# Layer 3's q and k on two 128x64 column tiles of the TensorE array, then copied to the row groups

## The chip, the cores and the metric

The kernel runs on one core of a Trainium2 chip. The metric is the device time of one execution in microseconds (us). The kernel before took 2777.07 us (median of three runs, 2775.02 to 2780.0); the profiled execution has a span of 2772.2 us. On this core TensorE (PE) multiplies, VectorE (DVE) and ScalarE (ACT) do the elementwise work and empty PSUM, GpSimd (POOL) does little, and SyncE (SP) issues nearly all DMAs. Each engine works through its own queue in order.

## The reference

Sixteen images of 256 channels and 32x32 points pass through four layers: a group norm with attention (layer 0), a gate made by two small convolutions (layer 1), group norm with attention again (layer 2), and an attention with narrow q and k (layer 3). All is float32. Layer 3 is the one that changes:

```python
def _L3_conv_ref(x, Wq, bq, Wk, bk, Wv, bv, gamma):
    B, C, H, W = x.shape                       # 16, 256, 32, 32
    N = H * W
    Dqk = Wq.shape[0]                          # 32
    scale = jnp.asarray(Dqk, x.dtype) ** (-0.5)
    xf = x.reshape(B, C, N)
    q = jnp.einsum('qc,bcn->bqn', Wq, xf) + bq[None, :, None]
    k = jnp.einsum('qc,bcn->bqn', Wk, xf) + bk[None, :, None]
    v = jnp.einsum('vc,bcn->bvn', Wv, xf) + bv[None, :, None]
    energy = jnp.clip(jnp.einsum('bqn,bqm->bnm', q, k) * scale, -10.0, 10.0)
    attn = jax.nn.softmax(energy, axis=-1)
    out = jnp.einsum('bcm,bnm->bcn', v, attn).reshape(B, C, H, W)
    return gamma[0] * out + x
```

## The kernel before

**Samples and lanes.** One sample (image) is one pass of the generator `sample`: attention of layer 0, the gate, attention of layer 2, then `clipped_attend`, which is layer 3. Even samples run in lane 0 and odd ones in lane 1. The two lanes are interleaved step by step (each `yield` is a step), with lane 1 a fixed number of steps behind, so that one lane's matrix products fill the waits of the other. The last part of each sample also carries `head` of the sample two further on: loading it and its first group norm (lines 118 to 145, among them two tiny products, `gm` on line 125 and `gv` on line 134, of which `gv` multiplies the small tile `d` from DVE line 131). While an even sample is in `clipped_attend`, lane 1 is in its layer 2; while an odd one is there, lane 0 has begun layer 0 of its next sample (the tiles `t`, lines 599 and 906).

**Order.** A tile framework places the instructions on the engines, keeps their order per engine, and adds the semaphores. It takes two accesses to one tile by different engines to be dependent more often than the data alone would ask. All PSUM tiles of the fast path come from one pool of eight banks (`bank`, 128 x 512 float32 each), used in turn.

**Matmuls in float32.** The trace shows each float32 matmul as two MATMUL records and two LDWEIGHTS records of the same shape; counts of the profile are counts of these records.

**Layer 3's q and k.** `w3` holds Wq, Wk and Wv side by side (columns 0 to 31, 32 to 63, 64 to 319) for the two halves `c` of the channels. At the start `fold3` makes `w3r` out of it, 128 columns wide: Wq twice and Wk twice. For each half `h` of the 1024 points (512 points), two matmuls over `c` on line 1041 (128 rows, 128 columns, 512 points) fill one bank: q in rows 0 to 31 and again in 32 to 63, k in 64 to 95 and again in 96 to 127. Four evictions follow: line 1050 (ACT) writes the 64 rows of q, with bias and scale, into rows 0 to 63 of the tile `t_qk`, then into rows 64 to 127; line 1057 (DVE) does so with k. ACT's and DVE's copies alternate in time, each waiting for the one before. The first copy of a sample also waits for DMA, because `t_qk` lies in the slot `t` of its lane, which the transfers of layer 2's output (`send`, line 515) still read.

So all four row groups of 32 partitions hold all of q and all of k. On line 1074 four products with 32 rows each, one per row group, run beside each other in the array: each takes another 128 keys and all 512 points of the half. ACT exponentiates their results (line 1083) and DVE clips them (line 1086). Between the copies and these products stand the values' products (line 525, evicted by ACT on line 1061) and the other lane's work. Lines 471 (bias strips), 906 (layer 0's `t`), 1061 and 1050 share ACT's queue; 131 (`d`), 136 (`ve`), 599, 638 to 641 (`tc`) and 1057 share DVE's.

Of the kernel before, what the change touches and what calls it, by code (L numbers as in the profile page):

```python
# [10 lines left out]
FP = mybir.dt.float32  # L11
I32 = mybir.dt.int32
AF = mybir.ActivationFunctionType
ALU = mybir.AluOpType
AX = mybir.AxisListType

P = 128
C = 256
CC = C // P
HW = 1024  # L20
NT = HW // P
HALF = 512
NH = HW // HALF
TPH = HALF // P
GROUP = 32
DQK = 32
G4 = P // DQK
PH = P // 2
STRIP = 32
NG = P // STRIP  # L30
# [11 lines left out]
OFFSET = 30  # L42


W_PLANES, W_GATE1, W_GATE2, W_SEND1 = 5, 3, 1, 8
W_NORM1, W_NORM2, W_NORM3, W_SEND2 = 6, 3, 2, 6
W_EXP, W_AV, W_AV3 = 2, 0, 0

S_W1, S_W2, S_B1, S_B2, S_GAMMA, NSCAL = 0, 18, 27, 28, 29, 30

# [150 lines left out]
def fast_path(nc, tc, k, bad, x, w_l0, w_l2, w_l3, qk_bias, v_bias, tap_idx, out):  # L201
# [7 lines left out]
    with ExitStack() as ctx:  # L209
        wts = ctx.enter_context(tc.tile_pool(name="wts", bufs=1))  # L210
# [12 lines left out]
        def bank(nm):  # L223
            return ps_m.tile([P, HALF], FP, tag="m", name=nm)
# [5 lines left out]
        def slot(what, lane, shape, nm):  # L230

            return qkvp.tile(shape, FP, tag=f"{what}_{lane}", name=f"{what}_{nm}", bufs=1)
# [26 lines left out]
        w3 = wts.tile([P, CC, 2 * DQK + C], FP, name="w3")  # L259
# [11 lines left out]
        bcol0, bcol2, bcol3 = (wts.tile([P, CC], FP, name=f"bcol{i}") for i in (0, 2, 3))  # L271
# [1 line left out]
        bstrip0, bstrip3 = (wts.tile([P, NS], FP, name=f"bstrip{i}") for i in (0, 3))  # L273

        qb = wts.tile([P, 1], FP, name="qb")
        for g in range(G4):
            i = g // 2
            nc.sync.dma_start(qb[g * DQK : (g + 1) * DQK, :], qk_bias[i * DQK : (i + 1) * DQK, :])

        def right_sums(engine, w, nm):  # L280

# [91 lines left out]
        def in_strips(col, strips, nm):  # L373

            ps = bank(f"strips_{nm}")
            for s in range(NG):
                nc.tensor.matmul(
                    ps[:STRIP, s * CC : (s + 1) * CC],
                    k.ident[:, s * STRIP : (s + 1) * STRIP],
                    col,  # L380
                    start=True,
                    stop=True,
                )
            for g in range(NG):
                nc.vector.tensor_copy(
                    strips[g * STRIP : (g + 1) * STRIP].rearrange("p (c s) -> p s c", c=CC),
                    ps[:STRIP, :NS].rearrange("p (s c) -> p s c", c=CC),
                )


        w3r = wts.tile([P, CC, P], FP, name="w3r")
        gam = k.sc[:, S_GAMMA : S_GAMMA + 1]

        def fold3():
            for g in range(G4):
                i = g // 2
                tc.keep_in_program_order(
                    nc.gpsimd.tensor_copy(
                        w3r[:, :, g * DQK : (g + 1) * DQK], w3[:, :, i * DQK : (i + 1) * DQK]
                    )  # L400
                )
            ps = bank("bias3")
            for c in range(CC):
                nc.tensor.matmul(
                    ps[:, CC : CC + 1],
                    w3r[:, c, :],
                    bcol2[:, c : c + 1],
                    start=(c == 0),
                    stop=(c == CC - 1),
                )  # L410
            for o in range(CC):
                for c in range(CC):
                    nc.tensor.matmul(
                        ps[:, o : o + 1],
                        w3[:, c, 2 * DQK + o * P : 2 * DQK + (o + 1) * P],
                        bcol2[:, c : c + 1],
                        start=(c == 0),
                        stop=(c == CC - 1),
                    )
            tc.keep_in_program_order(  # L420
                nc.vector.tensor_tensor(qb, ps[:, CC : CC + 1], qb, ALU.add)
            )
            nc.vector.tensor_scalar(qb[:PH], qb[:PH], DQK**-0.5, None, ALU.mult)
            nc.vector.tensor_tensor(bcol3, ps[:, :CC], vcol[:, 2, :], ALU.add)
            nc.vector.scalar_tensor_tensor(bcol3, bcol3, gam, bcol2, ALU.mult, ALU.add)
            in_strips(bcol3, bstrip3, "l3")
# [48 lines left out]
        def turn_strips(y, ts):  # L475

            part = y[:, :, ts].rearrange("p s t j -> p s (t j)")
            nc.vector.transpose(part, part)  # L478

        def by_strips(tokens):  # L480

            return tokens.rearrange("p (t g j) -> p g t j", t=TPH, g=NG)

        def half(h):
            return slice(h * TPH, (h + 1) * TPH)

        def in_pairs(y, ts, bias):

            return [
                functools.partial(add_to_strips, y, ts, bias, slice(s, s + 2))  # L490
                for s in range(0, NS, 2)
            ]
# [279 lines left out]
        def wait(steps):  # L772

            for _ in range(steps):
                yield
# [254 lines left out]
        def clipped_attend(xt, y, lane, b):  # L1030

            qk = slot("t", lane, [P, 2, HW], f"qk3_{b}")
            q, kk = qk[:, 0], qk[:, 1]
            vt = vts[lane]
            for h in range(NH):
                hs = slice(h * HALF, (h + 1) * HALF)
                ps = bank(f"qk3_{b}_{h}")
                for c in range(CC):  # L1040
                    nc.tensor.matmul(
                        ps.rearrange("p (g n) -> p g n", g=TPH),
                        w3r[:, c, :],
                        xt[:, half(h), c],
                        start=(c == 0),
                        stop=(c == CC - 1),
                    )

                for s in (slice(0, PH), slice(PH, P)):
                    nc.scalar.activation(  # L1050
                        by_strips(q[s, hs]),
                        ps[:PH, :].rearrange("p (g t j) -> p g t j", g=NG, t=TPH),
                        AF.Identity,
                        bias=qb[:PH],
                        scale=DQK**-0.5,
                    )
                    nc.vector.tensor_scalar(kk[s, hs], ps[PH:, :], qb[PH:], None, ALU.add)
                yield
                for t2 in range(h * TPH // 2, (h + 1) * TPH // 2):
                    ps, dst = values_of(xt, t2, w3[:, :, 2 * DQK :], vt, f"l3_{b}")  # L1060
                    nc.scalar.activation(dst, ps, AF.Copy, scale=gam)
                    yield
            tv = value_sums(lane)
            yield
            ri = small.tile([P, NT], FP, tag="ri", name=f"ri3_{b}")
            for h in range(NH):
                hs = slice(h * HALF, (h + 1) * HALF)
                e = expp.tile([P, NT, HALF], FP, tag="e", name=f"e3_{b}_{h}")
                for mg in range(NT // G4):
                    ss = [bank(f"s3_{b}_{h}_{mg}_{g}") for g in range(G4)]  # L1070
                    for g in range(G4):
                        mm = mg * G4 + g
                        gs = slice(g * DQK, (g + 1) * DQK)
                        nc.tensor.matmul(  # L1074
                            ss[g],
                            kk[gs, mm * P : (mm + 1) * P],
                            q[gs, hs],
                            start=True,
                            stop=True,
                        )  # L1080
                    for g in range(G4):
                        mm = mg * G4 + g
                        nc.scalar.activation(e[:, mm, :], ss[g], AF.Exp)  # L1083
                        if g % 2:
                            part = e[:, mm - 1 : mm + 1, :]
                            nc.vector.tensor_scalar(
                                part, part, EXP_MIN, EXP_MAX, ALU.max, ALU.min
                            )
                    yield from wait(W_EXP)
                yield from wait(W_AV3)  # L1090
                if b == B - 1 and h == NH - 1:
                    last = combp.tile([P, TPH, C], FP, tag="cb", name="last")
                    yield from weighted(e, vt, tv, y, ri, h, f"l3_{b}", last)
                    store_last(last, b, h)
                    continue
                yield from weighted(e, vt, tv, y, ri, h, f"l3_{b}")
                turn_strips(y, half(h))
                chores[lane].extend(in_pairs(y, half(h), bstrip3))
                chores[lane].append(functools.partial(store_tokens, y, b, h))
                yield  # L1100
            count(ri, f"l3_{b}")
# [59 lines left out]
        ps = bank("badp")  # L1161
# [317 lines left out]
```

## Time and profile before

| what | value |
|---|---|
| time, median of 3 | 2777.07 us |
| span of the profiled execution, granted TensorE clock | 2772.2 us, 0.996 |
| q/k matmuls, line 1041 | 128 records of 592 ns (median) |
| first copy on ACT, line 1050 | 64 x 680 ns |
| k's copy on DVE, line 1057 | 64 x 756 ns |
| products of q and k, line 1074 | 512 records |
| from first q/k matmul to first line-1074 product, even samples / odd samples | about 22.4 / 24.3 us |

A row of the groups gives line, engine, operation, what is written and read with shapes, the number of records, the time in which at least one of them ran, the mean length of one, and the idle time of the engine just before them with what ended it. In the timeline the columns are the start in us, the length of the merged run, engine, line, operation and count, and in brackets the idle time before it with the releaser.

### The profile page before, as it was taken

How to read it: one execution, taken by the hardware profiler on the slowest of the kernel's cores; microseconds unless marked ns; L12 is line 12 of the kernel's file. 1: busy time of each engine (PE TensorE's matmuls, PEld its weight loads, DVE VectorE, ACT ScalarE, POOL GpSimd, SP SyncE). 2: the span in 40 equal slices, each digit the busy share in tenths (PEclk: the TensorE clock that was granted, in tenths of full speed). 3: DMA queues.
4: the chain of work that ended last, by engine and by line, in shares of the span. 5: the costliest groups of instructions: out<-in, count | busy, mean ns of one | idle time of the engine just before them, and what ended most of it. 6: DMA issues, size and time to landing. Idle time of an engine off the chain costs nothing.

```text
span 2772.2 us, 46004 instructions
## 1 busy us (share of the span) xinstructions
PE 2701.7 (97%) x18102; PEld 2360.8 (85%) x18102; DVE 2096.8 (76%) x4045; ACT 1319.3 (48%) x2650; POOL 56.3 (2%) x118
## 2 busy tenths in 40 slices
PE   7999999999999999999999999999999999999997
PEld 6888888888988888888788887888888888888886
DVE  7887786877778777777777868778686887777765
ACT  3444355444554445544454445454444544445443
POOL 1000000000000000000000000000000000000000
PEclk9999999999999999999999999999999999999999
DMA  4011111011110120110201102111011011100101
GB/s 112 1 31 31 39 31 32 23 31 42 28 39 22 28 60 9 39 39 16 54 12 35 39 16 54 24 23 39 23 47 31 16 39 31 39 16 16 28 20 32
DMA packets 133790, 89.43 MB, mean 32 GB/s; under 512 B 17856, under 2 KB 132800, under 8 KB 133568
## 3 DMA queue, kind: packets, MB, share of 16 engines
q1 hardware_dynamic: 131696, 85.11, 12.5%
q8 instruction: 145, 2.38, 0.4%
q10 hardware_dynamic: 1872, 1.31, 0.2%
q14 instruction: 77, 0.63, 0.1%
HBM read 36.02 MB, written 16.78 MB: 19 GB/s over the span
## 4 chain that ended last, share of the span: by engine, by line
PE 69%; DVE 15%; ACT 6%; SPq 5%; DMA 2%; issue 2%; POOL 1%; ACTq 0%; DVEq 0%
PE b_l L567 12%; PE af_l L567 10%; PE c_l L567 10%; PE sb_l L567 9%; PE sc_l L567 6%; SPq L515 5%; PE sf_l L567 3%; PE sa_l L567 3%; PE vb_l L567 3%; PE tb_l L567 2%; PE vc_l L567 2%; ACT e_l L674 2%; PE tc_l L567 2%; DVE xr L722 2%; PE s L1074 2%
## 5 line engine op out<-in xcount | busy, mean ns | idle before, releaser
L674 ACT ACTIVATE e_l<-e_l 128x1024 f32<-128x1024 f32 x256 | 270.2, 1056 | 165.6 <-DVE e_l L599 164.5
L668 ACT COPY e_l<-sb_l 128x512 f32<-128x512 f32 x384 | 220.4, 582 | 170.3 <-PE sb_l L567 106.3
L567 PE MATMUL sb_l<-t_l,x 128*128 128x256 f32 x1024 | 266.1, 388 | 0.7 <-ACT e_l L668 0.7
L567 PE MATMUL b_l<-vt,e_l 128*128 128x128 f32 x2048 | 258.7, 277 | 0.9
L567 PEld LDWEIGHTS b_l<-vt,e_l 128*128 128x128 f32 x2048 | 244.8, 192 | 12.8 <-issue 7.7
L567 PEld LDWEIGHTS sb_l<-t_l,x 128*128 128x128 f32 x1024 | 179.8, 191 | 48.7 <-ACT e_l L668 13.6
L567 PE MATMUL c_l<-tv,cb_l 128*128 128x129 f32 x1536 | 187.2, 274 | 0.0
L599 DVE TENSOR_TENSOR e_l<-sc_l,e_l 128x512 f32<-128x512 f32 x128 | 88.1, 689 | 127.4 <-PE sc_l L567 125.3
L567 PEld LDWEIGHTS c_l<-tv,cb_l 128*128 128x128 f32 x1536 | 181.5, 191 | 1.6
L746 ACT COPY acc_l<-c_l 128x256 f32<-128x256 f32 x96 | 35.8, 373 | 271.5 <-DVE ri_l L745 178.4
L1083 ACT ACTIVATE e<-s 128x512 f32<-128x512 f32 x256 | 137.0, 605 | 54.5 <-PE s L1074 54.3
L567 PEld LDWEIGHTS af_l<-vt,e_l 128*128 128x128 f32 x1024 | 123.3, 192 | 38.0 <-ACT e_l L674 26.5
L567 PE MATMUL af_l<-vt,e_l 128*128 128x128 f32 x1024 | 131.6, 278 | 21.6 <-ACT e_l L674 21.6
L471 ACT ACTIVATE xr<-xr,bstrip 128x128 f32<-128x128 f32 (+1 forms) x376 | 139.3, 436 | 3.2 <-DVE xr L478 2.6
L567 PEld LDWEIGHTS af_l<-tv,e_l 128*128 128x128 f32 x1024 | 121.2, 192 | 19.4 <-issue 19.0
L599 DVE TENSOR_TENSOR e_l<-sf_l,e_l 128x512 f32<-128x512 f32 x128 | 88.5, 691 | 61.4 <-ACT e_l L668 61.2
L567 PE MATMUL sc_l<-tc_l,xs_l 128*128 128x256 f32 x512 | 133.0, 382 | 0.0
L567 PE MATMUL sb_l<-tc_l,xs_l 128*128 128x256 f32 x512 | 132.5, 381 | 0.5 <-ACT e_l L668 0.5
L567 PE MATMUL sa_l<-t_l,x 128*128 128x256 f32 x512 | 132.1, 381 | 0.0
L567 PE MATMUL sc_l<-t_l,xs_l 128*128 128x256 f32 x512 | 131.5, 379 | 0.0
L567 PE MATMUL c_l<-vt,e_l 128*128 128x129 f32 x1024 | 127.8, 277 | 3.7 <-ACT acc_l L746 3.6
L567 PE MATMUL sf_l<-tc_l,x 128*128 128x256 f32 x512 | 131.4, 379 | 0.0
(238 smaller groups left out, 5768.7 us busy)
## 6 DMA issues: line engine op xcount, KB each, us to landing
xr<-in_x_dram SPq DMA_DIRECT2D x64, 256.0 KB, 4.9
x<-t_z SPq DMA_DIRECT2D x256, 64.0 KB, 2.0
x<-t_l SPq DMA_DIRECT2D x512, 32.0 KB, 1.8
x<-in_x_dram SPq DMA_DIRECT2D x62, 256.0 KB, 4.1
out_dram<-xr SPq DMA_DIRECT2D x124, 128.0 KB, 2.3
raw_l<-in_w_l_dram SPq DMA_DIRECT2D x1, 1024.0 KB, 6.9
raw_l<-in_w_l_dram SPq DMA_DIRECT2D x2, 256.0 KB, 5.7
raw_l<-in_w_l_dram ACTq DMA_DIRECT2D x2, 256.0 KB, 5.6
```

The source lines that it names most:

```text
L471: nc.scalar.activation(y[:, s, ts], y[:, s, ts], AF.Identity, bias=bias[:, s : s + 1])
L515: queue.dma_start(dst[b * STRIP : (b + 1) * STRIP, g, halves], z[g * STRIP : (g + 1) * STRIP, halves, b],)
L567: mm = nc.tensor.matmul(out, left, right, start=fresh and m == 0 and (lone or i == 0), stop=(m == len(pairs) - 1), skip_group_check=True,)
L599: nc.vector.tensor_tensor(dst, src, dst, ALU.add)
L668: nc.scalar.copy(block(i, j), ps.rearrange("p (m n) -> p m n", m=2))
L674: nc.scalar.activation(e[:, m : m + 2, :], e[:, m : m + 2, :], AF.Exp)
L722: nc.vector.scalar_tensor_tensor(to, acc[:, i, :].rearrange("p (s j) -> p s j", j=STRIP), ri[:, t : t + 1], y[:, :, t, :], ALU.mult, ALU.add,)
L746: nc.scalar.copy(acc[:, hi, c2], c[:, :, :P])
L1074: nc.tensor.matmul(ss[g], kk[gs, mm * P : (mm + 1) * P], q[gs, hs], start=True, stop=True,)
L1083: nc.scalar.activation(e[:, mm, :], ss[g], AF.Exp)
```

## The change

The four column groups of the array are used as two tiles of 64 columns. Both hold Wq and Wk (64 columns, `w3[:, c, :64]`, no second set of weights), and each works on other points: tile 0 on the first 256 of the half, tile 1 on the last 256. So a half now has four matmuls with 64 columns and 256 points in place of two with 128 columns and 512 points. q and k come out once each, in rows 0 to 63 of the bank for the first points and 64 to 127 for the last. They are then copied to the row groups: q in full to each of the four groups (two copies of 32 rows and 256 points per group), and of k only the 128 keys that the group multiplies (one copy of 32 rows and 128 keys per group). ACT takes groups 0 and 2, DVE groups 1 and 3. The tile for k shrinks from 1024 to 256 columns. q's scale is multiplied into Wq and q's bias once at the start. The change is meant to take the doubled columns out of TensorE's work.

```diff
         qb = wts.tile([P, 1], FP, name="qb")
-        for g in range(G4):
-            i = g // 2
-            nc.sync.dma_start(qb[g * DQK : (g + 1) * DQK, :], qk_bias[i * DQK : (i + 1) * DQK, :])
+        for i in range(2):
+            nc.sync.dma_start(qb[i * PH : (i + 1) * PH], qk_bias)
...
         def fold3():
-            for g in range(G4):
-                i = g // 2
-                tc.keep_in_program_order(
-                    nc.gpsimd.tensor_copy(
-                        w3r[:, :, g * DQK : (g + 1) * DQK], w3[:, :, i * DQK : (i + 1) * DQK]
-                    )
-                )
+            tc.keep_in_program_order(
+                nc.vector.tensor_scalar(
+                    w3[:, :, :DQK], w3[:, :, :DQK], DQK**-0.5, None, ALU.mult
+                )
+            )
+            for i in range(2):
+                s = slice(i * PH, i * PH + DQK)
+                nc.vector.tensor_scalar(qb[s], qb[s], DQK**-0.5, None, ALU.mult)
             ps = bank("bias3")
...
-            qk = slot("t", lane, [P, 2, HW], f"qk3_{b}")
-            q, kk = qk[:, 0], qk[:, 1]
+            qk = slot("t", lane, [P, HW + NH * P], f"qk3_{b}")
+            q, kk = qk[:, :HW], qk[:, HW:]
             vt = vts[lane]
+            qt = TPH // 2
...
                 for c in range(CC):
-                    nc.tensor.matmul(
-                        ps.rearrange("p (g n) -> p g n", g=TPH),
-                        w3r[:, c, :],
-                        xt[:, half(h), c],
-                        start=(c == 0),
-                        stop=(c == CC - 1),
-                    )
-
-                for s in (slice(0, PH), slice(PH, P)):
-                    nc.scalar.activation(
-                        by_strips(q[s, hs]),
-                        ps[:PH, :].rearrange("p (g t j) -> p g t j", g=NG, t=TPH),
-                        AF.Identity,
-                        bias=qb[:PH],
-                        scale=DQK**-0.5,
-                    )
-                    nc.vector.tensor_scalar(kk[s, hs], ps[PH:, :], qb[PH:], None, ALU.add)
+                    for i in reversed(range(2)):
+                        g0 = h * TPH + i * qt
+                        nc.tensor.matmul(
+                            ps[i * PH : (i + 1) * PH, : qt * P].rearrange(
+                                "p (g n) -> p g n", g=qt
+                            ),
+                            w3[:, c, : 2 * DQK],
+                            xt[:, g0 : g0 + qt, c],
+                            start=(c == 0),
+                            stop=(c == CC - 1),
+                        )
+                for g in range(G4):
+                    gs = slice(g * DQK, (g + 1) * DQK)
+
+                    def take(dst, src, i, row):
+
+                        bias = qb[i * PH + row : i * PH + row + DQK]
+                        if g % 2:
+                            nc.vector.tensor_scalar(dst, src, bias, None, ALU.add)
+                        else:
+                            nc.scalar.activation(dst, src, AF.Identity, bias=bias)
+
+                    for i in range(2):
+                        rows_q = slice(i * PH, i * PH + DQK)
+                        src = ps[rows_q, : qt * P].rearrange("p (g t j) -> p g t j", g=qt, t=TPH)
+                        take(by_strips(q[gs, hs])[:, i * qt : (i + 1) * qt], src, i, 0)
+                    i, n = divmod(g, qt)
+                    src = ps[i * PH + DQK : (i + 1) * PH, n * P : (n + 1) * P]
+                    take(kk[gs, h * P : (h + 1) * P], src, i, DQK)
...
                         nc.tensor.matmul(
                             ss[g],
-                            kk[gs, mm * P : (mm + 1) * P],
+                            kk[gs, mg * P : (mg + 1) * P],
                             q[gs, hs],
```

The bias product of `fold3` (line 404) likewise goes to the two column tiles (four matmuls of one point in place of two).

More of the change, by code (lines that the diff above doesn't have):

```diff
@@ L42 @@
 OFFSET = 30
-W_PLANES, W_GATE1, W_GATE2, W_SEND1 = 5, 3, 1, 8
-W_NORM1, W_NORM2, W_NORM3, W_SEND2 = 6, 3, 2, 6
-W_EXP, W_AV, W_AV3 = 2, 0, 0
+W_PLANES, W_GATE1, W_GATE2, W_SEND1, W_NORM1, W_NORM2, W_NORM3, W_SEND2, W_EXP, W_AV, W_AV3 = 5, 3, 1, 8, 6, 3, 2, 6, 2, 0, 0
 S_W1, S_W2, S_B1, S_B2, S_GAMMA, NSCAL = 0, 18, 27, 28, 29, 30
@@ L388, in in_strips @@
                 )
-        w3r = wts.tile([P, CC, P], FP, name="w3r")
         gam = k.sc[:, S_GAMMA : S_GAMMA + 1]
         def fold3():
-            for g in range(G4):
-                i = g // 2
-                tc.keep_in_program_order(
-                    nc.gpsimd.tensor_copy(
-                        w3r[:, :, g * DQK : (g + 1) * DQK], w3[:, :, i * DQK : (i + 1) * DQK]
-                    )
-                )
+            tc.keep_in_program_order(
+                nc.vector.tensor_scalar(
+                    w3[:, :, :DQK], w3[:, :, :DQK], DQK**-0.5, None, ALU.mult
+                )
+            )
+            for i in range(2):
+                s = slice(i * PH, i * PH + DQK)
+                nc.vector.tensor_scalar(qb[s], qb[s], DQK**-0.5, None, ALU.mult)
             ps = bank("bias3")
             for c in range(CC):
-                nc.tensor.matmul(
-                    ps[:, CC : CC + 1],
-                    w3r[:, c, :],
-                    bcol2[:, c : c + 1],
-                    start=(c == 0),
-                    stop=(c == CC - 1),
-                )
+                for i in range(2):
+                    nc.tensor.matmul(
+                        ps[i * PH : (i + 1) * PH, CC : CC + 1],
+                        w3[:, c, : 2 * DQK],
+                        bcol2[:, c : c + 1],
+                        start=(c == 0),
+                        stop=(c == CC - 1),
+                    )
             for o in range(CC):
@@ L422, in fold3 @@
             )
-            nc.vector.tensor_scalar(qb[:PH], qb[:PH], DQK**-0.5, None, ALU.mult)
             nc.vector.tensor_tensor(bcol3, ps[:, :CC], vcol[:, 2, :], ALU.add)
@@ L1040, in clipped_attend @@
                 for c in range(CC):
-                    nc.tensor.matmul(
-                        ps.rearrange("p (g n) -> p g n", g=TPH),
-                        w3r[:, c, :],
-                        xt[:, half(h), c],
-                        start=(c == 0),
-                        stop=(c == CC - 1),
-                    )
-                for s in (slice(0, PH), slice(PH, P)):
-                    nc.scalar.activation(
-                        by_strips(q[s, hs]),
-                        ps[:PH, :].rearrange("p (g t j) -> p g t j", g=NG, t=TPH),
-                        AF.Identity,
-                        bias=qb[:PH],
-                        scale=DQK**-0.5,
-                    )
-                    nc.vector.tensor_scalar(kk[s, hs], ps[PH:, :], qb[PH:], None, ALU.add)
+                    for i in reversed(range(2)):
+                        g0 = h * TPH + i * qt
+                        nc.tensor.matmul(
+                            ps[i * PH : (i + 1) * PH, : qt * P].rearrange(
+                                "p (g n) -> p g n", g=qt
+                            ),
+                            w3[:, c, : 2 * DQK],
+                            xt[:, g0 : g0 + qt, c],
+                            start=(c == 0),
+                            stop=(c == CC - 1),
+                        )
[7 more added lines that the diff above has]
+                            nc.scalar.activation(dst, src, AF.Identity, bias=bias)
+                    for i in range(2):
+                        rows_q = slice(i * PH, i * PH + DQK)
[4 more added lines that the diff above has]
+                    take(kk[gs, h * P : (h + 1) * P], src, i, DQK)
                 yield
```

## The prediction

> **What bounds the kernel now.** I read the engines' shares first, then the chain.
>
> ```profile
> PE 2701.7 (97%) x18102; PEld 2360.8 (85%) x18102; DVE 2096.8 (76%) x4045; ACT 1319.3 (48%) x2650; POOL 56.3 (2%) x118
> ...
> PE 69%; DVE 15%; ACT 6%; SPq 5%; DMA 2%; issue 2%; POOL 1%; ACTq 0%; DVEq 0%
> ```
>
> TensorE is busy almost throughout, and the chain lies on it for 69%; the rest are places where it waited for DVE, ACT or a transfer. So a microsecond taken from PE's queue is gained, unless PE then waits at the next semaphore.
>
> Next the groups by shape, for what one half of q/k costs.
>
> ```profile
> L525 PE MATMUL vps_l<-w,x 128*128 128x256 f32 x512 | 120.7, 379 | 0.0
> ...
> L1074 PE MATMUL s<-t_qk 32*128 32x512 f32 x512 | 75.5, 639 | 0.4 <-DVE t_qk L1057 0.4
> ...
> L1041 PE MATMUL qk<-x,w3r 128*128 128x512 f32 x128 | 61.4, 602 | 1.3 <-issue 1.3
> ...
> L1057 DVE TENSOR_SCALAR t_qk<-qk,qb 64x512 f32<-64x512 f32 x64 | 48.4, 756 | 46.2 <-ACT t_qk L1050 44.4
> ...
> L1050 ACT ACTIVATE t_qk<-qk,qb 64x512 f32<-64x512 f32 x64 | 43.5, 680 | 77.4 <-DMA x<-t_l 43.0 <-DVE t_qk L1057 29.7 <-PE qk L1041 4.4
> ```
>
> Records overlap, so their mean is not their price; the price is start to start. Line 1074's 512 records of 639 ns fit into 75.5 us, over four at a time: products in separate row groups do run together.
>
> Last the timeline of an odd sample, for prices and for the wait that decides.
>
> ```profile
> 1015.97 1.88 PE L1041 MATMUL qk<-x,w3r 128*128 128x512 f32 x4
> ...
> 1017.69 1.02 PE L567 MATMUL tb_l<-x,m_l 128*128 128x512 f32 x2
> ...
> 1022.89 0.68 ACT L1050 ACTIVATE t_qk<-qk,qb 64x512 f32<-64x512 f32 x1 [3.39 <-DMA x<-t_l]
> ...
> 1026.57 0.35 PE L134 MATMUL gv_l<-d_l,gmat 128*128 128x2 f32 x2 [1.61 <-DVE d_l L131]
> ...
> 1030.38 1.12 PE L567 MATMUL tb_l<-x,m_l 128*128 128x512 f32 x2
> ```
>
> ```profile
> 1039.82 0.50 PE L567 MATMUL vc_l<-wvp_l,xs_l 128*128 128x128 f32 x3
> ...
> 1040.25 1.14 PE L1074 MATMUL s<-t_qk 32*128 32x512 f32 x8
> ...
> 1041.32 1.16 PE L567 MATMUL vb_l<-wvp_l,x 128*128 128x128 f32 x8
> ```
>
> One half of q/k occupies PE from 1015.97 to 1017.69: 1.72 us, 0.43 per record of 512 points. Records of 256 points follow each other at half that (line 525: eight in 1.89 less the last one's tail of 0.16, so 0.216 each). The second fence prices a change of tile shape. `vc` ends at 1040.32 and line 1074 at 1041.39: 1.07 us for two passes of 0.43, so 0.21 to go in. The eight `vb` records then end at 1042.48, 1.09 after line 1074, for 8 x 0.111: 0.20 to come out. A visit costs 0.40.
>
> **What the Trainium skill says.** "TensorEngine Tiling (Array Packing)", section Key Properties: changing the tiling mode drains TensorE. The trace agrees, with 0.2 us each way. "TensorE: Matmul & The Clock Gate", Part 3 (Measured speedup vs the span model): tiles in different column groups run concurrently, 2.38 times for three. The trace of before shows row groups doing so (4.3 at once) and no two column tiles together. The first page's section PSUM Bottleneck: tiling speeds TensorE but not the emptying of PSUM. Here that is the other side of the trade.
>
> **The change, part by part.**
>
> 1. *Matmuls.* Removed per half: 1.72 us. Added: four matmuls, eight records of 256 points. If the two tiles run together that is four passes, 4 x 0.216 = 0.86; if each record starts only when the one before it in the queue leaves its tile, five passes, 1.08; if they don't overlap at all, 1.72. I take 0.86, because the four row tiles do this in the trace, and the page says it of column tiles; both others stay in the range. 64-column weights instead of 128 can only shorten loads that are already hidden.
> 2. *Mode change.* New, 0.40 per half by the fence above. Sum on PE: 1.72 - 0.86 - 0.40 = 0.46 us saved per half, x32 = 14.7 us.
> 3. *ACT copies.* 512 elements take 680 ns. The slope comes from plain PSUM copies of 512 and 256 (582 and 373): 0.82 ns an element. So 256 takes 0.47 and 128 takes 0.36. Per half 4 x 0.47 + 2 x 0.36 = 2.6 against 2 x 0.68 = 1.36: +1.2, x32 = +40 us on an engine with 1450 us idle.
> 4. *DVE copies.* Slope 1.06 (accumulations of 512 and 256 from PSUM: 688 and 416). 256 takes 0.48, 128 takes 0.35; per half 2.6 against 1.51: +1.1, x32 = +36 us. DVE has 675 us idle, but in the windows from q/k to the first line-1074 product it is busy 15.25 of 22 us (even) and 18.06 of 24 (odd), ACT 10.19 and 13.33: room for the 2.3 us a sample that each gains.
> 5. *Waits.* The built program keeps the alternation, by group: three copies on ACT, three on DVE, three, three. The chain through one half grows from 2 x 0.68 + 2 x 0.76 = 2.9 us to about 5.2. Behind the waiting copies stand, on ACT, the values' evictions and layer 0's `t` (line 906), on which PE's next `tc` and `tb` products wait; on DVE, `ve`, `t` sums and the clips. The built order also puts the three `d` operations, which in odd samples stood between DVE's k copies, ahead of all of them: the `gv` wait above (14.4 us over eight samples in the list of waits) goes.
> 6. *Start.* `w3r`'s four copies off POOL, one small scaling on DVE, two more one-point matmuls in tile mode: under 1 us together, beside layer 0's first work.
>
> **Where the saving lands.** I walked the new queues with the old durations; back-to-back independent operations start some 0.08 us before the last ends, as the four bias strips of line 471 show (1.27 us for four of 0.395).
> *Odd samples:* the transfer still releases ACT at 6.9 us after the first q/k matmul. Two strips stand between the first copies; ACT comes to the second `t` copy so late that PE, without the `gv` wait, now waits about 0.9 at `tc`, and 1.0 again at the last `tb`, whose ACT copy ends near 13.5. `tb` then starts at 13.6 instead of 14.4 (1030.38 - 1015.97): 0.8 gained. The last q/k copy ends near 21.3, before PE wants it at 23.6.
> *Even samples:* the exponential that `af` needs follows the copies on ACT and ends near 11.1, when PE arrives; the reciprocal before the `c` products is no later than now. The whole 0.92 stays.
> *Last sample:* nothing else fills PE, the copies are the path, and I count 0.8 lost instead of 0.9 gained.
> Sum: 8 x 0.92 + 7 x 0.8 - 0.8 = 12.2 us, or 2777 - 12 = **2765 us**.
>
> **The rivals.**
> *Evictions take it back.* The chains are 2.3 us longer per half, and a slip of 1 us in my walks, on a queue whose order decides, takes the saving of a sample. For it: DVE waited 44.4 us for ACT's copies in the groups above and ACT 29.7 for DVE's, so the alternation is already a wait, with 75% DVE in odd windows. Against it: between q/k and its use stand 22 to 24 us. If half of the samples lose theirs and odd ones a little more, 2774 (2771 to 2779).
> *The column tiles don't run together.* Then PE pays 1.72 + 0.40 for 1.72: 0.40 x 32 = 12.8, plus about 1 at the end: 2791, **slower**. For it: nothing in the trace shows two column tiles at once; both read all 128 partitions of the moving data, while row tiles share them out. Against it: the page.
> *Five passes.* 0.24 per half, 7.7, less the last sample's 1.7: 2771. Part of the first case.
>
> **Numbers.** Saving as walked, with the five-pass form at its slow end: 0.58, 2758 to 2772. Evictions: 0.20, 2771 to 2779. No overlap: 0.22, 2783 to 2795. The range takes the first two and the near edge of the third: 2757 to 2786. Faster by over 0.2% (under 2771.5): nearly all of the first and a little of the second, 0.58. Within: 0.20. Slower: 0.22.
>
> **What would show it.** The new q/k row should have 256 records of about 0.38 us in some 34 us of busy time; 55 us would be the rival without overlap. From first q/k matmul to what follows 1.26 us. Copies near 0.47 and 0.36 on ACT, 0.48 and 0.35 on DVE. `gv` no longer waits for `d`; in odd samples waits for ACT's line-906 copies stand in its place. The distance from q/k to line 1074 falls to about 21.4 (even) and 23.6 (odd). I am wrong if the tiles run one after another, if copies of 32 rows cost as much as those of 512 points, or if `tc` and `tb` wait longer for ACT than 0.9 and 1.0.

## The result, and the profile after

The changed kernel takes **2789.56 us** (median of four runs, 2788.07 to 2791.29) where the kernel before takes 2776.7 (2775.02 to 2780.0): 1.0045 times as long, with a 95% interval of 1.0028 to 1.0062. It is slower by some 12.9 us; 2765 had been forecast. The profiled spans are 2787.2 and 2772.2 us.

The page of the changed kernel, in its engine shares and its chain of waits:

```profile
PE 2701.9 (97%) x18234; PEld 2358.9 (85%) x18234; DVE 2126.3 (76%) x4175; ACT 1361.3 (49%) x2778; POOL 58.5 (2%) x114
...
PE 65%; DVE 17%; ACT 7%; SPq 5%; issue 2%; DMA 2%; POOL 1%; ACTq 0%; DVEq 0%
```

TensorE is on the chain for 65% in place of 69%; DVE and ACT have taken what it lost. SPq and DMA still hold 5% and 2%, as before. That pair, the issue and the flight of transfers, turns out to be the key to the case.

The groups by shape, after (line, engine, operation, shapes, count | busy us, mean ns | idle before, what ended it):

```profile
L1087 PE MATMUL s<-t_qk 32*128 32x512 f32 x512 | 86.7, 644 | 0.7 <-DVE t_qk L1060 0.7
L1060 DVE TENSOR_SCALAR t_qk<-qk,qb 32x256 f32<-32x256 f32 x128 | 61.2, 478 | 63.3 <-ACT t_qk L1062 61.2
L1062 ACT ACTIVATE t_qk<-qk,qb 32x256 f32<-32x256 f32 x128 | 59.3, 463 | 56.2 <-DMA x<-t_l 45.9 <-DVE t_qk L1060 8.4
L1044 PE MATMUL qk<-x,w 128*64 128x256 f32 x256 | 36.2, 406 | 1.9 <-DMA x<-t_l 1.9
```

The last row answers the forecast's first question: 256 records of 406 ns in 36.2 us of busy time, so the two column tiles do run together (one after the other they would have needed 55). Each copy costs what was expected, 463 and 478 ns for 256 columns. But DVE now waits 61.2 us for ACT's copies, where it waited 44.4, and ACT's first copies still wait for the transfer that reads the slot `t` (45.9 us; before 43.0).

The timeline of an odd sample after (start, length, engine, operation, count; in brackets the idle time before, and what ended it):

```profile
2382.87 1.08 PE L1044 MATMUL qk<-x,w 128*64 128x256 f32 x8
...
2389.87 0.47 ACT L1062 ACTIVATE t_qk<-qk,qb 32x256 f32<-32x256 f32 x1 [4.08 <-DMA x<-t_l]
...
2391.10 0.28 PE L132 MATMUL gv_l<-d_l,gmat 128*128 128x2 f32 x2
...
2393.10 0.68 ACT L903 ACTIVATE t_l<-tc_l,tb_l 128x512 f32<-128x512 f32 x1
2393.80 1.31 ACT L1062 ACTIVATE t_qk<-qk,qb 32x256 f32<-32x256 f32 x3
2393.83 1.13 PE L564 MATMUL tc_l<-xs_l,m_l 128*128 128x512 f32 x2 [1.49 <-ACT t_l L903]
...
2396.74 0.68 ACT L903 ACTIVATE t_l<-tb_l,tb_l 128x512 f32<-128x512 f32 x1
...
2397.47 1.13 PE L564 MATMUL tb_l<-x,m_l 128*128 128x512 f32 x2 [1.49 <-ACT t_l L903]
```

A half of q/k takes about 1.0 us from its start to the next product, and `gv` waits no more. But ACT comes to the `t` copies late, because q/k's copies stand before them in its queue, and TensorE waits 1.49 us twice. The last `tb` starts 14.6 us after the first q/k product; before it was 14.4. What the array saved is gone.

An even sample after shows the third such wait, which was not there before: ACT makes three copies in 1.31 us, only then the exponential, and `af` waits for that.

```profile
2310.97 1.31 ACT L1062 ACTIVATE t_qk<-qk,qb 32x256 f32<-32x256 f32 x3
...
2312.30 1.06 ACT L671 ACTIVATE e_l<-e_l 128x1024 f32<-128x1024 f32 x1
...
2313.41 1.61 PE L564 MATMUL af_l<-vt,e_l 128*128 128x128 f32 x12 [0.66 <-ACT e_l L671]
```

A fourth loss shows as no idle time of TensorE. The first row of the groups has the products of q and k busy for 86.7 us, where it was 75.5, though a record is hardly longer (644 ns, 639 before). In odd samples the second set of four products starts together no more. Before:

```profile
1042.41 1.32 PE L1074 MATMUL s<-t_qk 32*128 32x512 f32 x8
```

After:

```profile
1046.06 2.23 PE L1087 MATMUL s<-t_qk 32*128 32x512 f32 x8
...
1046.40 0.69 DVE L596 TENSOR_TENSOR vt<-vc_l,vt 128x512 f32<-128x512 f32 x1
```

One product runs alone; the other three start 1.1 us later, by the profile's releaser when DVE has emptied a PSUM bank (`vc`). Before, DVE did that 25.5 us after q/k's start in the sample that the prediction shows; now it comes to it at 27.6, behind its copies and what these delayed. The profile's list of waits has seven waits for this operation of DVE, 5.3 us in all, one in each odd sample but the last. In a typical odd sample the first product of line 1087 starts 24.45 us after q/k, 0.17 later than before; this set then adds 0.9.

The sum over the two profiled runs, by the starts of the first q/k products: even sample to the next odd one +0.44 us on average (eight times, 3.5), odd to the next even one +1.08 (seven times, 7.6), from the last sample's q/k to the end +4.7, and the first even sample 0.8 earlier. Together 15.0, the difference of the spans.

### What the copies wait for

The length of these waits differs from sample to sample, and one quantity explains it: the time from the first q/k product until the transfer releases the first copy on ACT. In the kernel before, another odd sample than the one that the prediction shows:

```profile
1362.44 0.68 ACT L1050 ACTIVATE t_qk<-qk,qb 64x512 f32<-64x512 f32 x1 [4.61 <-DMA x<-t_l]
...
1366.13 0.55 PE L134 MATMUL gv_l<-d_l,gmat 128*128 128x2 f32 x2 [2.83 <-DVE d_l L131]
```

The product started at 1354.3 there, so the release came at 8.14 us and `gv` waited 2.83. In the sample of the prediction it was 6.92 and 1.61.

| kernel, wait | release after q/k's start -> wait of TensorE, us |
|---|---|
| before, odd samples, `gv` | 6.92 -> 1.61; 7.42 -> 2.11; 7.58 -> 2.28; 8.14 -> 2.83 |
| after, even samples, `af` | 6.72 -> 0.67; 7.21 -> 1.16; 7.61 -> 1.55; 7.64 -> 1.58; 7.84 -> 1.78 |
| after, odd samples, `tc` | 6.99 -> 1.48; 7.50 -> 1.99; 7.89 -> 2.38 |

Each row is a straight line of slope one: wait = release less 5.31 before, less 6.06 (even) and 5.51 (odd) after. The rows give the different values; all seven odd samples before, the first seven even ones after and the seven odd ones fit. The last even one, where nothing is loaded ahead any more, lies off with 6.63 -> 1.02. So before as well as after, the chain begins at the transfer out of slot `t`. The change lengthened what hangs behind it, twelve copies in place of four.

### The profile page after: what moved, and what is told of

Its sections match the earlier page's. It is cut to its first block, busy times and chain, and to the rows that moved or that the text cites. A ratio compares the mean times of both kernels' runs of the same rounds, so it can differ in the third digit from the quotient of the medians.

```text
span 2787.2 us, 46518 instructions
## 1 busy us (share of the span) xinstructions
PE 2701.9 (97%) x18234; PEld 2358.9 (85%) x18234; DVE 2126.3 (76%) x4175; ACT 1361.3 (49%) x2778; POOL 58.5 (2%) x114
## 3 DMA queue, kind: packets, MB, share of 16 engines
q10 hardware_dynamic: 1872, 1.31, 0.2%
## 4 chain that ended last, share of the span: by engine, by line
PE 65%; DVE 17%; ACT 7%; SPq 5%; issue 2%; DMA 2%; POOL 1%; ACTq 0%; DVEq 0%
PE b_l L564 12%; PE af_l L564 10%; PE c_l L564 10%; PE sb_l L564 9%; PE sc_l L564 6%; SPq L512 5%; PE sf_l L564 3%; PE sa_l L564 3%; PE vb_l L564 2%; DVE t_qk L1060 2%; PE tb_l L564 2%; ACT e_l L671 2%; PE vc_l L564 2%; DVE xr L719 2%; PE tc_l L564 1%
## 5 line engine op out<-in xcount | busy, mean ns | idle before, releaser
L564 PEld LDWEIGHTS sb_l<-t_l,x 128*128 128x128 f32 x1024 | 180.0, 191 | 48.4 <-ACT e_l L665 13.6
L1060 DVE TENSOR_SCALAR t_qk<-qk,qb 32x256 f32<-32x256 f32 (+1 forms) x192 | 83.7, 436 | 64.2 <-ACT t_qk L1062 61.2
```

The lines of the kernel that those rows point to most:

```text
L564: mm = nc.tensor.matmul(out, left, right, start=fresh and m == 0 and (lone or i == 0), stop=(m == len(pairs) - 1), skip_group_check=True,)
L1060: nc.vector.tensor_scalar(dst, src, bias, None, ALU.add)
```

## The experiments

The theory: the array's part of the change gains, and the copies lose it again, because they start late, at the transfer's release, and then hold up others in ACT's and DVE's queues. The rival: TensorE's own costs (visits to another tile shape) or the start. Ratios are to the kernel before, each with its 95% interval.

**1 and 5. Column tiles with three copies.** The replication is left out: three copies of all 128 rows, on one bank and in slot `t` as before.

```diff
-                for g in range(G4):
-                    ... twelve copies of 32 rows
+                nc.scalar.activation(by_strips(q[:, hs])[:, :qt], src, AF.Identity, bias=qb)
+                nc.vector.tensor_scalar(by_strips(q[:, hs])[:, qt:], src, qb, None, ALU.add)
+                nc.vector.tensor_scalar(kk[:, h * P : (h + 1) * P], ps[:, :P], qb, None, ALU.add)
```

> The column tiles of the changed kernel stay; the twelve copies of a half shrink to three that take all 128 rows where they lie (one of 256 columns on ACT, one of 256 and one of 128 on DVE), so layer 3's attention reads wrong q and k: this run leaves the replication out. Theory (the array's part of the change gains, the twelve copies that ACT and DVE hand to each other lose it again): the start of a q/k half to the next product stays near 1.0 us against 1.72 before, nothing waits for the copies, and the time falls to about 2762 (2756 to 2768), 15 us under the kernel before. Rival (the visits to the other tile shape, or something at the start, cost what the total shows): it stays near 2789, at best 2783.

Measured: 7969.61 us. Without the replication, sums of layer 3 left the bounds up to which the fast route holds, and the kernel went on to its general route, so that this time says nothing. The trace of the fast route does: samples of a lane lie 335.5 us apart, where it was 339.3 before and 340.9 after. Run again with the kernel's flag held at zero:

> As e1, but with the final flag set to zero. In e1 the wrong q and k broke the kernel's bounds on the softmax sums, so that after the fast route it took its general route too (7970 us), and its time could not be compared; only its trace could: samples of a lane 335.5 us apart, against 339.3 before and 340.9 after. Left out: the replication of q and k and the flag. The theory (array gains, copies lose) in its form of now: eight pairs at 335.5 and a tail of some 138 us give 2743 (2738 to 2750). The rival (TensorE's own cost) was at 2783 to 2789.

Measured: 2747.24 us, 0.9897 (0.9881 to 0.9914). With few copies the kernel is 28 us faster than before, although they wait for the transfer as ever. Some 16 of this would be the products' by the estimate below; the rest, some 12, fits three short copies that hold up others less than the four long ones did (`gv` waits 0.85 to 1.46 us in odd samples, before 1.59 to 2.83), but was not priced by itself. The rival falls: visits to the tile shape and start are all in this run. The groups of this run also show that a copy of 128 rows costs what one of 32 does (463 and 478 ns above):

```profile
L1057 DVE TENSOR_SCALAR t_qk<-qk,qb 128x256 f32<-128x256 f32 x32 | 15.4, 480 | 37.2 <-ACT t_qk L1054 37.2
L1054 ACT ACTIVATE t_qk<-qk,qb 128x256 f32<-128x256 f32 x32 | 15.2, 474 | 45.3 <-DMA x<-t_l 45.0 <-PE qk L1044 0.3
```

**2. The copies alone.** Old products, new copies.

```diff
-                for c in range(CC):
-                    for i in reversed(range(2)):
-                        ... 64 columns, 256 points, tile i
+                for c in range(CC):
+                    nc.tensor.matmul(ps..., w3r[:, c, :], xt[:, half(h), c], ...)
```

> The other half of the change alone: q and k by the old two 128x128 products of 512 points, then the twelve copies of the changed kernel, of the same sizes and engines (q's scale in the weights). Theory: the copies' cost stands alone, without the array's gain: the 12.9 us that the changed kernel lost plus the 15 or so that the array gained, so about 2803 (2795 to 2810). Rival (the loss is TensorE's, by the change of tile shape): about 2777, no slower than 2782. If the copies' waits are partly the doing of products that finish sooner, between: 2785 to 2795.

Measured: 2797.81 us, 1.0072 (1.0059 to 1.0085). With the old products, twelve copies in place of four cost 21 us (2797.8 less 2776.6; in the traces 25.5, of which 4.4 lie ahead of the first q/k product), within the expected range. The changed kernel lies 7 or 8 below that (1.0072 against 1.0045). This is a difference of two totals, not the price of the tiles, because the two kernels wait in different places. Here the built order leaves the `d` operations behind DVE's first copies, and `gv` waits 2.1 to 2.9 us in all seven odd samples:

```profile
2060.78 0.35 PE L132 MATMUL gv_l<-d_l,gmat 128*128 128x2 f32 x2 [2.11 <-DVE d_l L129]
```

Each of these waits is followed by 3.41 us in which TensorE is granted half its clock (last section), a loss of at most 11.8 us in all; ahead of the last sample the kernel before has two such stretches (at most 3.4) and the changed one three (5.0). So part of the 21 us is the clock's answer to the waits.

**3. Two banks.** Each column tile fills its own bank; ACT empties one, DVE the other.

```diff
-                ps = bank(f"qk3_{b}_{h}")
+                pp = [bank(f"qk3_{b}_{h}_{i}") for i in range(2)]
...
-                        if g % 2:
+                    if i:
                         nc.vector.tensor_scalar(dst, src, bias, None, ALU.add)
```

> The changed kernel with the two column tiles in two PSUM banks in place of one: ACT takes all six copies out of tile 0's bank, DVE all six out of tile 1's, so neither waits for the other; twelve copies as before, same sizes. Theory in its narrow form (the handing to and fro makes the chain long: 5.2 us per half become about 2.8): waits of tc and tb for ACT and of af for the exponential shrink by about 1 us each, and the time is about 2768 (2760 to 2776). Rival (the work of twelve copies on the two queues is what delays the others, whatever the order): it stays at 2785 to 2791. A side effect may spoil it: in even samples the built order now puts DVE's six copies, and their wait for the transfer, between d's first and second step, and gv would wait for them.

Measured: 2820.11 us, 1.0155 (1.0141 to 1.0168), the slowest of all and outside both expectations. The timeline of an even sample says why:

```profile
1300.83 0.16 DVE L127 TENSOR_TENSOR d_l<-mv_l,gms_l 128x2 f32<-128x2 f32 x1
...
1303.25 2.63 ACT L1059 ACTIVATE t_qk<-qk,qb 32x256 f32<-32x256 f32 x6 [2.03 <-DMA x<-t_l]
1303.31 2.71 DVE L1057 TENSOR_SCALAR t_qk<-qk,qb 32x256 f32<-32x256 f32 x6 [2.33 <-DMA x<-t_l]
...
1306.06 0.16 DVE L128 TENSOR_TENSOR d_l<-d_l 128x2 f32<-128x2 f32 x1
...
1307.15 0.35 PE L132 MATMUL gv_l<-d_l,gmat 128*128 128x2 f32 x2 [3.86 <-DVE d_l L129]
```

The chain of the copies is halved as meant: six on each engine, side by side, done in 2.7 us. But now DVE waits for the transfer too, with the second step of `d` behind the copies, and `gv` waits 3.86 us. All samples but the last two have such a wait, of 2.6 to 4.4 us, and after twelve of these fourteen TensorE runs at half its clock, a loss of at most 23 us. The two theories of the expectation could not be told apart here; the side effect it named decided. What follows is that the wait for the transfer must go before the chain is worth shortening.

**6 and 7. A tile of their own for q and k.** The change had shrunk q and k from 2048 columns to 1280, and one such tile for both lanes fits, if some tiny tiles get two buffers in place of four. Nothing is transferred out of it.

```diff
-            qk = slot("t", lane, [P, HW + NH * P], f"qk3_{b}")
+            qk = qkvp.tile([P, HW + NH * P], FP, tag="qk", name=f"qk3_{b}", bufs=1)
```

> The changed kernel with q and k in a tile of their own, one for both lanes, in place of the slot t (a few small tiles get two buffers in place of four to make room): the first copy no longer waits for the transfers that still read the slot, and can start some 2 us after the first q/k product in place of 6.9. Twelve copies, one bank, the same alternation. If the collision in time is the cause (copies that are released late fall on what tc, tb and af wait for), 2766 (2758 to 2776). If the length of the alternating chain is the cause whenever it runs, or the mere work, 2783 to 2790.

Measured: 2746.72 us, 0.9899 (0.9883 to 0.9916): 43 us less than the changed kernel, by this one edit, and below the expected range. The waits of `tc`, `tb`, `af` and of the three late products are gone from the trace (that set of four takes 1.32 us again); `gv` waits 0.5 us in even samples and 0.16 in odd ones. No half-clock stretch is left ahead of the last sample. The order that the framework builds for ACT and DVE changes with this edit as well, as it did in 2 and 3; no run holds it fixed. With the two banks of experiment 3 added:

> e6 and e3 together: own tile and two banks, so the copies start early and ACT's six run beside DVE's six. In e3 the two banks halved the chain as meant (six copies on each engine, all done in 2.7 us from a common start), but DVE's copies waited for the transfer with d's second step behind them, and gv cost 3.3 us in even and 2.9 us in odd samples; here nothing waits for the transfer, and d stands behind copies that are done early. If that reading of e3 is right: faster than before, 2755 (2748 to 2764), and no gv wait over 0.5 us. If two banks are bad in themselves (one bank more of eight in use): 2790 or more.

Measured: 2734.77 us, 0.9855 (0.9839 to 0.9872), the best of all, below the expected range, and so better than both kernels. Its page and the timeline of an odd sample:

```profile
PE 2678.4 (98%) x18234; PEld 2351.0 (86%) x18234; DVE 2127.7 (78%) x4175; ACT 1358.1 (50%) x2778; POOL 52.4 (2%) x114
...
PE 89%; ACT 4%; DVE 4%; issue 1%; DMA 0%; SPq 0%; POOL 0%; ACTq 0%; DVEq 0%
```

```profile
2340.15 1.08 PE L1044 MATMUL qk<-x,w 128*64 128x256 f32 x8
...
2341.36 2.63 ACT L1059 ACTIVATE qk<-qk,qb 32x256 f32<-32x256 f32 x6 [0.74 <-PE qk L1044]
...
2348.38 0.28 PE L132 MATMUL gv_l<-d_l,gmat 128*128 128x2 f32 x2
...
2349.46 1.02 PE L564 MATMUL tc_l<-xs_l,m_l 128*128 128x512 f32 x2
...
2352.11 1.12 PE L564 MATMUL tb_l<-x,m_l 128*128 128x512 f32 x2
```

ACT's and DVE's busy times are those of the changed kernel, 1358 and 2128 us: the same copies, no dearer, only begun 1.2 us after the product in place of 7.0. `gv`, `tc` and `tb` wait for nothing that the view would show (no brackets), the last `tb` starts 12.0 us after the first product in place of 14.6, and SPq and DMA have left the chain: from 5% and 2% to 0%.

**8 and 9. What the column tiles are worth now.** Old products in an own tile: with the twelve copies of experiment 6, and with the fewest that they allow.

```diff
+                for s in (slice(0, PH), slice(PH, P)):
+                    nc.scalar.activation(by_strips(q[s, hs]), ps[:PH, :]..., AF.Identity, bias=qb[:PH])
+                for g in range(G4):
+                    ... k: one copy of 32 rows and 128 keys, on DVE
```

> e6 with the old products: two 128x128 products of 512 points for a half, twelve copies, one bank, own tile (Wq and Wk stand twice in w3 itself, and three small tiles get one buffer, to make room). Against e6 it prices the column tiles where the copies are early. From the traces: products shorter by 0.85 us a half, visits to the tile shape 0.35 a half, so 0.50 x 32 = 16 us. If all of that counts once the copies are out of the way: 2763 (2757 to 2769). If TensorE's part never mattered and the early copies are all of e6's gain: 2747. If e6 gained by the column tiles alone: 2785 or more.

> The old products in an own tile with the fewest copies that they allow: q by two copies of 64 rows and 512 points on ACT as before, k by four copies of 32 rows and 128 keys on DVE. The chain of a half is 2 x 0.68 + 4 x 0.35 = 2.8 us in place of 5.2. If an early start is what counts and the copies' number little: near e8, 2760 (2754 to 2766). If their number counts as well: as much better than e8 as e7 is than e6 (12 us), 2751. In both cases it should stay above e7's 2735, because the products cost 16 us more; if it comes below 2740, the column tiles are not worth having.

Measured: 2757.07 us, 0.9934 (0.992 to 0.9947), and 2750.78 us, 0.9909 (0.9893 to 0.9924). Both faster than before: the own tile is worth 41 us to the old products as well (2797.8 less 2757.1), so most of the gain is not the array's. Against 8, the column tiles of experiment 6 gain 10 us by the medians (4 to 16 by the two intervals; 13.7 by the profiled spans), where 16 were expected. By the starts of the samples in the two traces it is 0.92 us for each of the fifteen samples before the last, where 1.0 was expected; the last sample gives 1.1 back. So TensorE's arithmetic holds within what these runs can tell. Experiment 7 lies 16.0 below 9 (9 to 21), but there the copies differ as well, twelve from two banks and six from one. What an own tile would give to the four old copies was not tried; they need 2048 columns in place of 1280.

**4 and 10. Two controls.** The scale in the weights alone, in the kernel before; and the small tiles' buffers of 6 alone, in the changed kernel.

```diff
+            nc.vector.tensor_scalar(w3[:, :, :DQK], w3[:, :, :DQK], DQK**-0.5, None, ALU.mult)
...
-                        scale=DQK**-0.5,
```

```diff
-    r1 = small.tile([STRIP, STRIP], FP, tag="r1", name=f"r1_{nm}")
+    r1 = small.tile([STRIP, STRIP], FP, tag="r1", name=f"r1_{nm}", bufs=2)
```

> The kernel before with q's scale multiplied into its weights and bias once, nothing else. All theories but one: 2777, within 2 us. If the start of the change costs something: 2780 or more, and layer 3's first samples begin later.

> A control for e6 and e7: the changed kernel as it is, with q and k in the slot t, only with the small tiles' buffers cut to two as in e6. If the buffers have no part in it: 2789.5, within 3 us. If they helped by themselves: under 2780.

Measured: 2776.26 us, 0.9999 (0.9991 to 1.0007), and 2791.16 us, 1.0049 (1.0034 to 1.0064). Neither has a part in the result.

| products | copies a half | tile, banks | us |
|---|---|---|---|
| old (before) | 4 | slot `t`, 1 | 2777 |
| old (2) | 12 | slot `t`, 1 | 2797.8 |
| old (8) | 12 | own, 1 | 2757.1 |
| old (9) | 6 | own, 1 | 2750.8 |
| column tiles (after) | 12 | slot `t`, 1 | 2789.6 |
| column tiles (3) | 12 | slot `t`, 2 | 2820.1 |
| column tiles (6) | 12 | own, 1 | 2746.7 |
| column tiles (7) | 12 | own, 2 | 2734.8 |

## Why the prediction was wrong

**Matmuls: right.** 0.86 us a half was taken, and the two tiles do overlap. **Mode change: a little too dear.** From end to end a visit costs 0.15 us to go in and 0.20 to come out, 0.35 in place of 0.40. The products thus save 0.85 - 0.35 = 0.50 a half, 16 us in place of 14.7; experiments 6 and 8 show 0.92 a sample, or 0.46 a half. What the Trainium skill says in "TensorEngine Tiling (Array Packing)", section Key Properties (a change of mode drains), is borne out by these 0.15 and 0.20 us, and what its section PSUM Bottleneck says (tiling does nothing for the emptying of PSUM) by the copies: 463 and 478 ns beside the tiles, 465 and 477 beside the old products of experiment 2.

**Copies, and the order of `d`: right.** The lengths came out at 463 and 359 ns (ACT), 478 and 351 (DVE), and the wait of `gv` for `d` left the odd samples.

**Where the saving lands: wrong, and this is the failed step.** Its terms, against the starts of the samples:

| term | predicted | measured |
|---|---|---|
| even samples (8) | -0.92 each | +0.44 each |
| odd samples (7) | -0.8 each | +1.08 each |
| last sample | +0.8 | +4.7 |
| sum, with the start | -12.2 | +15.0 (profiled spans) |

*Even samples:* the exponential that `af` needs was to end 11.1 us after q/k's start. It ended at 11.8 (2312.30 + 1.06 less 2301.54) in the best samples, and later by as much as the release was late, up to 13 (the release came at 6.6 to 7.8 us, 7.1 on average). The walk had an overlap of 0.08 us between neighbouring operations, taken from the bias strips. q/k's copies don't overlap: three, with means that sum to 0.463 + 0.463 + 0.359 = 1.285, take 1.31, and up to the exponential no operation of this queue starts before the one ahead has ended. Eight joins at 0.08 are 0.64, nearly the 0.7 by which the best samples were late.

*Odd samples:* 0.9 and 1.0 us were forecast for `tc` and `tb`; both measured 1.49 in five of seven samples, and `tc` 1.99 and 2.38 in the first two. In the sample above ACT ended the copy for `tc` 10.9 us after q/k's start and the one for `tb` at 14.5, where 13.5 was forecast: of the sixteen joins from the first q/k copy to there seven overlap, by some 0.1, and the others not at all, 0.5 us together, where 0.08 at each would be 1.28. So `tb` started at 14.6, not at 13.6. (The prediction names two strips between the first copies; the built queue has two more and one of the values' evictions ahead of the copy for `tc`. It doesn't say whether the walk counted these.) The other 0.9 us are those of the set of four products that waited for a bank. The walk followed the copies to their use, at 24.45 in place of 23.6, and no further; when DVE empties the banks that the next products need is a term that it doesn't have. -0.8 + 1.0 + 0.9 makes the measured 1.1.

*Last sample:* this was the coarsest guess and the largest error for one sample. The first copy is released at about 6.5 us in both kernels. Before, the last of k's copies:

```profile
2718.94 0.68 ACT L1050 ACTIVATE t_qk<-qk,qb 64x512 f32<-64x512 f32 x1 [5.88 <-DMA x<-t_l]
...
2726.21 0.76 DVE L1057 TENSOR_SCALAR t_qk<-qk,qb 64x512 f32<-64x512 f32 x1 [0.75 <-ACT t_qk L1050]
```

and after:

```profile
2729.24 0.46 ACT L1062 ACTIVATE t_qk<-qk,qb 32x256 f32<-32x256 f32 x1 [2.77 <-DMA x<-t_l]
...
2739.70 1.35 DVE L1060 TENSOR_SCALAR t_qk<-qk,qb 32x256 f32<-32x256 f32 x3
```

From the first to the end of the last it is 8.0 us before (2726.97 less 2718.94) and 11.8 after. With no other lane to fill the gap, these 3.8 us are most of the 4.7. TensorE also runs at half its clock for 10.24 us from 2738.26 on, where the kernel before has one stretch of 3.41 ahead of its end; how the rest divides was not worked out.

**The rivals.** "Evictions take it back" named the mechanism and was priced at 2774: at 14.7 for the array it charged the copies and their waits 12 us (2774 less 2777 - 14.7), the forecast itself 2.5; experiment 2 found 21, and beside the faster products it is 29 (12.9 + 16). "No overlap" would have given nearly the measured time for a wrong reason; the row of L1044 excludes it. This is why a time alone doesn't confirm a theory.

**What had been readable before.** The prediction took the transfer's release for a fixed mark at 6.9 us and moved the queues behind it. Views of the kernel before said more: SPq and DMA on the chain with 5% and 2%, ACT's 43.0 us of waiting for `x<-t_l`, and `gv` waits that rise one for one with the release. Work that hangs behind the last event of a chain has no slack, however idle its engine is on average.

## What to carry to other kernels

Before pricing longer evictions by an engine's idle share, ask what releases the first of them; if it is a transfer still reading the destination's old contents, every added copy is on the path, and another buffer may be worth more than the change itself: 41 to 43 us here, against 10 to 16 for the array. Then follow the queue past the use of the copies, to the banks that the same engine empties for others. When a change shrinks a tile, look whether the smaller tile now fits somewhere that nothing else holds. Shortening a chain by spreading it over two engines can lose if the second engine then waits for the same late event with small, urgent work behind it.

## What the runs showed of the hardware

Two column tiles of 64 columns with float32 operands ran together: eight records of 256 points in about 1.0 us, entry included. ACT and DVE emptied two banks at once without slowing each other: six copies in 2.63 and 2.71 us, side by side, with means of 463 and 480 ns for 256 columns, as from one bank in turn (463 and 478). A copy of 256 columns took the same for 32 rows and for 128 (463 and 474 ns on ACT, 478 and 480 on DVE).

A long wait of TensorE can cost more than its length, and where it falls decides. In each trace the stretches at half clock start on one grid of 3.41 us and, the one at the program's end apart, last 3.41 us or a multiple of it. Four windows of experiment 3 on this grid (us, PE's busy time and records, clock, DMA share, GB/s), around a `gv` wait of 2.63 us in an odd sample, then around one of 3.65 in an even sample:

```profile
2417.05:2420.46 3.41, 0.78 (x4) 1.00 0.00 0
2420.46:2423.87 3.41, 3.41 (x8) 0.50 0.00 0
1645.63:1649.05 3.42, 1.45 (x7) 1.00 0.05 14
1649.05:1655.87 6.82, 5.14 (x43) 1.00 0.00 0
```

The first wait lies within one window, which leaves TensorE idle for 2.63 us of it, and the next window runs at half clock: a record of 512 points took up to 1061 ns there, 592 elsewhere. The second, longer wait is cut by a border of the grid into parts of 1.97 and 1.68, and nothing follows. Over the traces of both kernels and of experiments 2 to 10, between the first q/k product and the last sample, all 22 windows at full clock with over 2.01 us idle were followed by a half-clock stretch, three of the seven with 1.78 to 2.01, and none with less. The Trainium skill, "TensorE: Matmul & The Clock Gate", section "What's actually happening", tells of a free-running window of some 3.4 us and of half rate after an idle one; the traces agree with the window, but here some 2 us of idleness within it was enough.
